# The MLP of a four-layer vision kernel by Strassen's product, in blocks of 256 pixels

## Chip, cores, metric

One core of one Trainium2 chip. The metric is the device time of one execution in microseconds, median of several runs. A ratio is the mean time of one kernel's fast runs over that of the other's fast runs of the same rounds, so it is not quite the ratio of the medians.

## The reference, cut to what matters

Four layers on `x` of shape (2, 512, 32, 32), all in f32: a deformable attention block with an MLP, then three attention layers. The change touches the MLP, which ends the first layer:

```python
xn2 = _bn(x, bn2_g, bn2_b)
h1 = jax.nn.gelu(jnp.einsum('bchw,oc->bohw', xn2, mlp_w1) + mlp_b1[None, :, None, None], approximate=False)
return x + jnp.einsum('bchw,oc->bohw', h1, mlp_w2) + mlp_b2[None, :, None, None]
```

512 channels go to 2048 and back, for 2 x 1024 = 2048 pixels.

## The kernel before

The MLP runs in four halves of 512 pixels. Channels lie on the 128 partitions, so 512 channels are CC = 4 chunks and 2048 are 16. `wa` and `wb` hold the two weights. `norm` is the group norm of layer 1, advanced in steps between MLP groups, so that layer 1 can start at once.

```python
xn = normed(0, 0)                                  # GpSimd: 4 tensor_scalar
for b in range(B):
    for half in range(2):
        ...
        h1 = one.tile([P, HID // P, HALF], F32, name="hid")
        for m in range(HID // P):                  # 16 groups of 4 matmuls
            ph = ps.tile([P, HALF], F32, name="ph")
            for k in range(CC):
                nc.tensor.matmul(
                    ph, w1[:, k, m * P : (m + 1) * P], xn_now[:, k, :], start=(k == 0), stop=(k == CC - 1)
                )
            nc.scalar.activation(h1[:, m, :], ph, AF.Gelu, bias=col("mlp_b1", m))
            if b == 1 and m % 4 == 3:
                advance(norm)
        ...
        for m in range(CC):                        # 4 groups of 16 matmuls
            pp = ps.tile([P, HALF], F32, name="pp2")
            for k in range(HID // P):
                nc.tensor.matmul(
                    pp, w2[:, k, m * P : (m + 1) * P], h1[:, k, :], start=(k == 0), stop=(k == HID // P - 1)
                )
            nc.vector.scalar_tensor_tensor(
                xs[b][:, m, n], pp, col("mlp_b2", m), xs[b][:, m, n], ALU.add, ALU.add
            )
            nc.sync.dma_start(out=x_d[b, m, :, n], in_=xs[b][:, m, n])
```

Around it, the pool `chan` has 9 buffers of 4 KB a partition in SBUF, the core's working memory. Each holds 128 channels of one image: of the normalised images of layers 1 and 2 (four buffers an image) or of the attention heads' outputs. The fold weights `g2`, `v2` and the bias row `vbias` have a place from the start.

Of the kernel before, what the change touches and what calls it, by code (L numbers as in the profile page):

```python
# [11 lines left out]
F32 = mybir.dt.float32  # L12
AF = mybir.ActivationFunctionType
ALU = mybir.AluOpType
# [4 lines left out]
P = 128  # L19
B, C, H, W = 2, 512, 32, 32  # L20
HW = H * W
CC = C // P
HALF = 512
# [5 lines left out]
HID = 4 * C  # L29
# [50 lines left out]
def kernel(ctx: ExitStack, tc: tile.TileContext, a: dict, out: bass.AP):  # L80
    nc = tc.nc
# [10 lines left out]
    def col(name, i=0, n=1):  # L92
        lo = _PC_AT[name][0] + i
        return pc[:, lo : lo + n]
# [7 lines left out]
    xs = []  # L102
# [26 lines left out]
    def advance(steps, n=1):  # L129
        for _ in range(n):  # L130
            next(steps, None)

    def accumulate(pm, pairs):
        for k, (w, m) in enumerate(pairs):
            nc.tensor.matmul(pm, w, m, start=(k == 0), stop=(k == len(pairs) - 1))  # L135
# [759 lines left out]

            attend([(k[:DH], q[:DH])], 1.0, vT, [(m * P, P) for m in range(CC)], store)

    def layers(f, g2, v2, t2_b, o2_b):


        f.enter_context(in_order(tc))
        small = f.enter_context(tc.tile_pool(name="small", bufs=2))
        keep = f.enter_context(tc.tile_pool(name="keep", bufs=1))
        chan = f.enter_context(tc.tile_pool(name="chan", bufs=9))
        ps_m = f.enter_context(tc.tile_pool(name="ps_m", bufs=2, space=PSUM))


        vb = keep.tile([P, 3, CC], F32, name="vb")
        with nc.allow_non_contiguous_dma("1536 numbers"):
            nc.sync.dma_start(out=vb, in_=a["vb"].rearrange("l (k p) -> p l k", p=P))  # L910
        vbias = keep.tile([P, C], F32, name="vbias")
        nc.sync.dma_start(out=vbias, in_=a["vb"][0].partition_broadcast(P))
        gb3 = keep.tile([P, CC], F32, name="gb3")
        nc.vector.tensor_scalar(gb3, vb[:, 2, :], col("gamma3"), None, ALU.mult)
        ones = keep.tile([P, P], F32, name="ones1")
# [60 lines left out]
        wb = wb_stack.enter_context(tc.tile_pool(name="wb", bufs=1, side="right"))  # L976
        (w2,) = load_w(wb, "wb", [a["mlp_w2"]])
        with ExitStack() as mlp:
            one = mlp.enter_context(tc.tile_pool(name="mlp1", bufs=1, side="right"))
            two = mlp.enter_context(tc.tile_pool(name="mlp2", bufs=2, side="right"))  # L980
            ps = mlp.enter_context(tc.tile_pool(name="mlp_ps", bufs=3, space=PSUM))

            def normed(b, half):
                n = slice(half * HALF, (half + 1) * HALF)
                xn = two.tile([P, CC, HALF], F32, name="xn2")
                for cc in range(CC):
                    nc.gpsimd.tensor_scalar(  # L987
                        xn[:, cc, :], xs[b][:, cc, n], s2[:, cc : cc + 1], col("bn2_b", cc), ALU.mult, ALU.add
                    )
                return xn  # L990

            xn = normed(0, 0)
            for b in range(B):
                for half in range(2):
                    n = slice(half * HALF, (half + 1) * HALF)
                    xn_now = xn
                    if (b, half) != (B - 1, 1):
                        xn = normed(*divmod(2 * b + half + 1, 2))
                    h1 = one.tile([P, HID // P, HALF], F32, name="hid")
                    for m in range(HID // P):  # L1000
                        ph = ps.tile([P, HALF], F32, name="ph")
                        for k in range(CC):
                            nc.tensor.matmul(  # L1003
                                ph, w1[:, k, m * P : (m + 1) * P], xn_now[:, k, :], start=(k == 0), stop=(k == CC - 1)
                            )
                        nc.scalar.activation(h1[:, m, :], ph, AF.Gelu, bias=col("mlp_b1", m))  # L1006
                        if b == 1 and m % 4 == 3:
                            advance(norm)
                    if (b, half) == (B - 1, 1):
                        qkv1, proj1 = load_w(wa, "wa", [a["qkv1_w"], a["proj1_w"]])  # L1010
                    for m in range(CC):
                        pp = ps.tile([P, HALF], F32, name="pp2")
                        for k in range(HID // P):
                            nc.tensor.matmul(  # L1014
                                pp, w2[:, k, m * P : (m + 1) * P], h1[:, k, :], start=(k == 0), stop=(k == HID // P - 1)
                            )
                        nc.vector.scalar_tensor_tensor(  # L1017
                            xs[b][:, m, n], pp, col("mlp_b2", m), xs[b][:, m, n], ALU.add, ALU.add
                        )
                        nc.sync.dma_start(out=x_d[b, m, :, n], in_=xs[b][:, m, n])  # L1020
                if b == 0:
                    for w, j in ((g2, 0), (v2, 1)):
                        nc.sync.dma_start(out=w, in_=fold_d[j])
        drain(norm)


# [87 lines left out]
            return r  # L1114

        wb_stack.close()

        vp = f.enter_context(tc.tile_pool(name="vp", bufs=1))
        pp_ = f.enter_context(tc.tile_pool(name="pp", bufs=4))
# [40 lines left out]
        for i in range(65):  # L1160
# [17 lines left out]
            if late is not None:  # L1178

                lb, lm, ls, lp = late  # L1180
                if ls == 0:
                    pv = ps_v.tile([P, HW], F32, name="pv")
                    if lm == 0 and lb == 1:
                        vT = new_v()
                        drain(values(qkv1[:, :, 2 * C : 3 * C], h1s[1], vT, bias=vbias))
                for half in range(2):
                    n = slice(half * HALF, (half + 1) * HALF)
                    for part in range(2):
                        lo = lm * P + part * 64
                        nc.tensor.matmul(  # L1190
                            pv[part * 64 : part * 64 + 64, n],
                            vT[:, ls, lo : lo + 64],
                            lp[:, part, n],
                            start=(ls == 0),
                            stop=(ls == 7),
                        )
                if ls == 1:
                    acc = accp.tile([P, 2, HW], F32, name="acc")
                    summed(acc, lp, p_first)
                elif ls > 1:  # L1200
                    summed(acc, lp, None)
                p_first = lp
                if ls == 7:
                    o = chan.tile([P, HW], F32, name="o", tag="chan")
                    nc.vector.tensor_copy(o, pv)
                    drain(dividing)
                    dividing = divide(o, acc)
                    os_[lb].append(o)
                    if lm == 3 and lb == 0:
                        more = chain([None] * 6, add_projection(xs[0], proj1, "proj_b", os_[0]))  # L1210
# [52 lines left out]
        for b in range(B):  # L1263
# [5 lines left out]
            ps = []  # L1269
# [68 lines left out]
    t2_b, o2_b = [const.tile([P, CC], F32, name=name) for name in ("t2_b", "o2_b")]  # L1338
    with ExitStack() as l0:
        w1 = layer0(l0, fold_d, t2_b, o2_b)  # L1340
    with tc.tile_pool(name="fold2", bufs=1) as pool, ExitStack() as fast:
        g2, v2 = [pool.tile([P, CC, C], F32, name=name) for name in ("g2", "v2")]
        layers(fast, g2, v2, t2_b, o2_b)
    bad = nc.values_load(flag[0:1, 0:1], min_val=0, max_val=P)
    with tc.If(bad != 0):
        with ExitStack() as g:
# [86 lines left out]
```

## Time and profile before

| | before |
|---|---|
| median of 4 runs (lowest to highest) | 3701.33 us (3700.52 to 3702.98) |
| TensorE busy, share of the span | 99% |
| MLP, first matmul to first matmul after it | 440.1 us |
| MLP matmul records (see below), us apart | 1024, 0.429 |
| VectorE, ScalarE busy in the MLP | 19 us, 50 us |

One f32 matmul stands in the trace as two records with a weight load each. A record lasts longer (592 ns at 512 pixels) than the distance to the next one's start (429 ns), so neighbours overlap. What a record costs is the distance between starts. The lines themselves are in the prediction below.

### The profile page before, as it was taken

How to read it: one execution, taken by the hardware profiler on the slowest of the kernel's cores; microseconds unless marked ns; L12 is line 12 of the kernel's file. 1: busy time of each engine (PE TensorE's matmuls, PEld its weight loads, DVE VectorE, ACT ScalarE, POOL GpSimd, SP SyncE). 2: the span in 40 equal slices, each digit the busy share in tenths (PEclk: the TensorE clock that was granted, in tenths of full speed). 3: DMA queues.
4: the chain of work that ended last, by engine and by line, in shares of the span. 5: the costliest groups of instructions: out<-in, count | busy, mean ns of one | idle time of the engine just before them, and what ended most of it. 6: DMA issues, size and time to landing. Idle time of an engine off the chain costs nothing.

```text
span 3702.9 us, 37416 instructions
## 1 busy us (share of the span) xinstructions
PE 3677.3 (99%) x15234; PEld 1339.8 (36%) x15234; DVE 2369.3 (64%) x2317; ACT 1588.3 (43%) x1964; POOL 500.1 (14%) x189
## 2 busy tenths in 40 slices
PE   9999999999999999999999999999999999999999
PEld 4333333333333333333333334444433333444443
DVE  6998998998996998998999950000046356030222
ACT  3656566566664566666656541110134233111111
POOL 1123122122131011131132300000001000000000
PEclk9999999999999999999999999999999999999999
DMA  4010112111010010010001001000100000000000
GB/s 150 16 21 17 18 24 62 16 21 18 19 23 12 16 21 18 20 22 16 21 18 24 18 1 54 9 32 12 57 0 1 1 1 1 14 1 0 6 29 24
DMA packets 96853, 78.42 MB, mean 21 GB/s; under 512 B 10657, under 2 KB 84769, under 8 KB 95905
## 3 DMA queue, kind: packets, MB, share of 16 engines
q1 hardware_dynamic: 96528, 75.41, 8.2%
q8 instruction: 123, 2.02, 0.2%
q10 hardware_dynamic: 144, 0.52, 0.0%
q14 instruction: 58, 0.47, 0.0%
HBM read 64.12 MB, written 10.75 MB: 20 GB/s over the span
## 4 chain that ended last, share of the span: by engine, by line
PE 98%; DVE 1%; ACT 0%; DMA 0%; issue 0%; POOL 0%; SPq 0%; DVEq 0%; POOLq 0%; ACTq 0%
PE z L454 48%; PE sim L476 6%; PE pw L135 6%; PE ph L1003 6%; PE pp L1014 6%; PE pm L1038 5%; PE pmv L135 5%; PE score L1142 3%; PE score L135 3%; PE pv L1190 3%; PE ppr L1069 2%; PE pp L561 2%; PE pf L135 1%; PE pk L135 0%; DVE acc L1080 0%; PE pv L539 0%
## 5 line engine op out<-in xcount | busy, mean ns | idle before, releaser
L454 PE MATMUL z<-h,cpb_w 128*64 128x512 f32 x8192 | 1791.0, 594 | 3.5 <-ACT qpad L273 3.5
L462 ACT ACTIVATE h<-z,b2h 128x1024 f32<-128x1024 f32 x1024 | 1140.0, 1115 | 840.6 <-PE z L454 834.7
L436 DVE CUSTOM_DVE_ANT_1 h<-tab,tab 128x1024 f32<-128x1024 f32 x1024 | 1220.3, 1232 | 113.8 <-PE z L454 113.3
L454 PEld LDWEIGHTS z<-h,cpb_w 128*64 128x64 f32 x8192 | 574.3, 137 | 1183.0 <-issue 1085.1
L467 DVE SCALAR_TENSOR_TENSOR h<-h,turn,h 128x1024 f32<-128x1024 f32 x512 | 688.0, 1344 | 5.3 <-ACT h L462 5.3
L421 POOL TENSOR_SCALAR tab<-tab,pc 128x512 f32<-128x512 f32 x63 | 294.8, 4679 | 1621.7 <-DMA tab<-slog_d 1309.4
L1017 DVE SCALAR_TENSOR_TENSOR x<-pp,pc,x 128x512 f32<-128x512 f32 x16 | 12.0, 752 | 375.7 <-PE pp L1014 375.7
L476 PE MATMUL sim<-h,w 128*32 128x512 f32 x2048 | 234.4, 595 | 0.7 <-DVE h L467 0.7
L135 PE MATMUL pw<-p,vT 128*128 128x512 f32 x512 | 221.8, 593 | 1.3 <-DVE y L1248 1.3
L1003 PE MATMUL ph<-xn,wa 128*128 128x512 f32 x512 | 220.9, 592 | 1.4 <-POOL xn L987 1.4
L1014 PE MATMUL pp<-hid,wb 128*128 128x512 f32 x512 | 220.4, 592 | 0.0
L1143 ACT ACTIVATE p<-score 128x1024 f32<-128x1024 f32 x144 | 139.5, 1021 | 156.7 <-PE score L1142 156.7
L1080 DVE TENSOR_TENSOR acc<-acc,p 128x2048 f32<-128x2048 f32 x56 | 129.6, 2314 | 105.1 <-ACT p L1143 57.8
L1006 ACT ACTIVATE hid<-ph,pc 128x512 f32<-128x512 f32 x64 | 44.0, 687 | 332.6 <-PE ph L1003 332.6
L965 POOL TENSOR_SCALAR hc<-x,sc,sh 128x1024 f32<-128x1024 f32 x16 | 29.6, 1862 | 902.2 <-DVE sh L961 870.1
L1082 DVE TENSOR_TENSOR acc<-p 128x2048 f32<-128x2048 f32 x12 | 27.5, 2291 | 183.4 <-ACT p L1277 110.0
L1003 PEld LDWEIGHTS ph<-xn,wa 128*128 128x128 f32 x512 | 97.0, 190 | 123.2 <-issue 120.5
L1014 PEld LDWEIGHTS pp<-hid,wb 128*128 128x128 f32 x512 | 97.3, 190 | 122.5 <-issue 122.5
L135 PEld LDWEIGHTS pw<-p,vT 128*128 128x128 f32 x512 | 97.0, 190 | 122.6 <-issue 121.0
L422 POOL TENSOR_SCALAR tab<-tab,pc 128x512 f32<-128x512 f32 x63 | 129.1, 2049 | 20.8 <-DMA tab<-slog_d 20.6
L1142 PE MATMUL score<-q,k 64*128 64x512 f32 x512 | 127.2, 615 | 0.0
L1038 PE MATMUL pm<-hc,wa 128*64 128x512 f32 x512 | 122.4, 603 | 0.0
(217 smaller groups left out, 2050.1 us busy)
## 6 DMA issues: line engine op xcount, KB each, us to landing
tab<-slog_d SPq DMA_DIRECT2D x128, 256.0 KB, 6.5
wa<-in_qkv_w SPq DMA_DIRECT2D x8, 768.0 KB, 6.7
xt<-in_xt SPq DMA_DIRECT2D x8, 512.0 KB, 3.9
wa<-in_mlp_w SPq DMA_DIRECT2D x4, 1024.0 KB, 15.9
wb<-in_mlp_w SPq DMA_DIRECT2D x16, 256.0 KB, 5.4
x_d<-x SPq DMA_DIRECT2D x16, 256.0 KB, 2.0
out<-x SPq DMA_DIRECT2D x16, 256.0 KB, 2.0
wa<-in_proj_w SPq DMA_DIRECT2D x8, 256.0 KB, 8.8
```

What stands on the lines that cost most here:

```text
L135: nc.tensor.matmul(pm, w, m, start=(k == 0), stop=(k == len(pairs) - 1))
L421: engine.tensor_scalar(tabs[0], tabs[0], col("cpb_w1", 0), col("cpb_b1"), ALU.mult, ALU.add)
L436: nc.vector._custom_dve(TENSOR_ADD_SAT, out=h1, in0=tx[:, quad, ri, :].unsqueeze(1).to_broadcast([P, H, W]), in1=ty[:, quad, ri, :].unsque ...
L454: nc.tensor.matmul(z[point * 64 : point * 64 + 64, n], cpb_w2[:, part * 64 : part * 64 + 64], h1s[point][:, n], start=True, stop=True,)
L462: nc.scalar.activation(h2, z, AF.Relu, bias=b2h[:, part : part + 1])
L467: nc.vector.scalar_tensor_tensor(parts[0], parts[0], turn, parts[1], ALU.mult, ALU.add)
L476: nc.tensor.matmul(sim[quad * 32 : quad * 32 + 32, n], w3[:, lo : lo + 32], h2[:, n], start=(r == 0 and j < 4), stop=False,)
L1003: nc.tensor.matmul(ph, w1[:, k, m * P : (m + 1) * P], xn_now[:, k, :], start=(k == 0), stop=(k == CC - 1))
L1014: nc.tensor.matmul(pp, w2[:, k, m * P : (m + 1) * P], h1[:, k, :], start=(k == 0), stop=(k == HID // P - 1))
L1038: nc.tensor.matmul(pm[at : at + wide], w[:, k, lo + at : lo + at + wide], h[k][:, n], start=(k == 0), stop=(k == CC - 1),)
L1142: nc.tensor.matmul(sc[:, part, :], ks[part][r, left[part]], qs[part][r, n], start=True, stop=True)
L1143: nc.scalar.activation(p[:, :, n], sc, AF.Exp, scale=scale)
```

## The change

Strassen's product (in Winograd's form) multiplies 2 x 2 block matrices with 7 block products in place of 8, for additions on other engines. The intent is to give TensorE, which is busy all the time, one eighth less MLP work. Blocks are 256 pixels wide, halved into 128, so each moving operand is 128 wide.

- The sums of weights are formed once on VectorE, in place where possible, while the first block is multiplied plainly.
- The order of the second product is chosen for the wait between the two products: product 1 is taken for both output halves over seven chunks, and the chunk that comes last only then.
- Room is made in SBUF: `chan` goes to 4 buffers, the heads' outputs get 5 of their own, and `g2`, `v2`, `vbias` are loaded after the MLP.

The diff, cut to its core:

```diff
-        chan = f.enter_context(tc.tile_pool(name="chan", bufs=9))
+        chan = f.enter_context(tc.tile_pool(name="chan", bufs=4))
...
+            def lefts(w, name):          # sums of a weight's blocks
+                    engine.tensor_tensor(t1[c], a21[c], a22[c], ALU.add)
+                    engine.tensor_tensor(t2[c], t1[c], a11[c], ALU.subtract)
+                    engine.tensor_tensor(a21[c], a11[c], a21[c], ALU.subtract)
+                    engine.tensor_tensor(t4[c], a12[c], t2[c], ALU.subtract)
...
+            def rights(v, name):         # sums of the pixels' blocks: 4 tensor_tensor alike
...
+                at = {1: a[:, 0], 2: a[:, 1], 6: a[:, 2], 3: a[:, 3], 4: b[:, 0], 5: b[:, 1], 7: b[:, 2]}
...
+            def combined(pms, p1, lower):
+                nc.vector.tensor_tensor(upper, a[:, 1:3], twice(p1), ALU.add)
+                nc.vector.tensor_tensor(u, b[:, 1:3], twice(upper[:, 1]), ALU.add)
+                nc.vector.tensor_tensor(lower, b[:, 0:2], twice(u[:, 1]), ALU.add)
+                nc.vector.tensor_tensor(upper[:, 1], a[:, 3], u[:, 0], ALU.add)
...
+            for blk in range(1, NBLK):
...
+                for c in range(MC + 1):
+                    if c < MC:
+                        pms = products(left1, right1, slice(c * P, (c + 1) * P), (1, 2, 6, 7, 5, 4, 3))
+                        p1 = first_of(pms)
+                    if c:
+                        activated(c - 1, upper)
+                    if c < MC:
+                        upper = combined(pms, p1, hid[:, MC + c, :].rearrange("p (j n) -> p j n", j=2))
+                    if c:
+                        form_right2(slice(c - 1, c))
+                    if b == 1 and c % 4 == 3:
+                        advance(norm)
...
+                both = [products(left2, right2, cols[c], ()) for c in range(2)]
+                for ks in (range(MC - 1), range(MC - 1, MC)):
+                    for c in range(2):
+                        for k in ks:
+                            nc.tensor.matmul(both[c][0][:, 0], left2[0][:, k, cols[c]], right2[0][:, k, :], ...)
+                for c in range(2):
+                    products(left2, right2, cols[c], (2, 6, 7, 5, 4, 3), both[c])
...
+        fold2 = f.enter_context(tc.tile_pool(name="fold2", bufs=1))   # vbias, g2, v2: loaded after the MLP
+        outs = f.enter_context(tc.tile_pool(name="outs", bufs=5))
```

`a` and `b` are two banks of PSUM, the memory that TensorE writes its sums to, with room for four results of 128 pixels each. There are three of each, and each is one tile of the program. A *group* is one pass of `c`: the seven products for one pair of column blocks, 14 matmuls or 28 records. The *seam* is the place where the second product of a block follows on the first.

More of the change, by code (lines that the diff above doesn't have):

```diff
@@ L896, in general, with layers @@
             attend([(k[:DH], q[:DH])], 1.0, vT, [(m * P, P) for m in range(CC)], store)
-    def layers(f, g2, v2, t2_b, o2_b):
+    def layers(f, fold_d, t2_b, o2_b):
         f.enter_context(in_order(tc))
@@ L910, in layers @@
             nc.sync.dma_start(out=vb, in_=a["vb"].rearrange("l (k p) -> p l k", p=P))
-        vbias = keep.tile([P, C], F32, name="vbias")
-        nc.sync.dma_start(out=vbias, in_=a["vb"][0].partition_broadcast(P))
         gb3 = keep.tile([P, CC], F32, name="gb3")
@@ L981, in layers, with blocks @@
             ps = mlp.enter_context(tc.tile_pool(name="mlp_ps", bufs=3, space=PSUM))
-            def normed(b, half):
-                n = slice(half * HALF, (half + 1) * HALF)
-                xn = two.tile([P, CC, HALF], F32, name="xn2")
+            BLK = 256
+            PX = BLK // 2
+            def blocks(v, k, n):
+                return [
+                    [v[:, i * k // 2 : (i + 1) * k // 2, j * n // 2 : (j + 1) * n // 2] for j in range(2)]
+                    for i in range(2)
+                ]
@@ new lines, in lefts, with form @@
+            def lefts(w, name):
+                k, n = w.shape[1:]
+                (a11, a21), (a12, a22) = blocks(w, k, n)
+                t1, t2, t4 = [one.tile([P, k // 2, n // 2], F32, name=f"{name}s{i}") for i in (1, 2, 4)]
+                def form(engine, cols):
+                    c = (slice(None), slice(None), cols)
+                    engine.tensor_tensor(t1[c], a21[c], a22[c], ALU.add)
+                    engine.tensor_tensor(t2[c], t1[c], a11[c], ALU.subtract)
+                    engine.tensor_tensor(a21[c], a11[c], a21[c], ALU.subtract)
+                    engine.tensor_tensor(t4[c], a12[c], t2[c], ALU.subtract)
+                return (a11, a12, t4, a22, t1, t2, a21), form
@@ new lines, in rights, with form @@
+            def rights(v, name):
+                k, n = v.shape[1:]
+                (b11, b12), (b21, b22) = blocks(v, k, n)
+                t1, t2, t4 = [one.tile([P, k // 2, n // 2], F32, name=f"{name}t{i}") for i in (1, 2, 4)]
+                def form(chunks):
+                    c = (slice(None), chunks, slice(None))
+                    nc.vector.tensor_tensor(t1[c], b12[c], b11[c], ALU.subtract)
+                    nc.vector.tensor_tensor(t2[c], b22[c], t1[c], ALU.subtract)
+                    nc.vector.tensor_tensor(b12[c], b22[c], b12[c], ALU.subtract)
+                    nc.vector.tensor_tensor(t4[c], b21[c], t2[c], ALU.subtract)
+                return (b11, b21, b22, t4, t1, t2, b12), form
@@ new lines, in product, with products @@
+            def product(pm, i, left, right, cols):
+                l, r = left[i - 1], right[i - 1]
+                accumulate(pm, [(l[:, k, cols], r[:, k, :]) for k in range(l.shape[1])])
+            def products(left, right, cols, some, pms=None):
+                if pms is None:
+                    pms = [ps.tile([P, 4, PX], F32, name=f"pm{i}") for i in "ab"]
+                a, b = pms
+                at = {1: a[:, 0], 2: a[:, 1], 6: a[:, 2], 3: a[:, 3], 4: b[:, 0], 5: b[:, 1], 7: b[:, 2]}
+                for i in some:
+                    product(at[i], i, left, right, cols)
+                return pms
@@ new lines, in combined, with twice @@
+            def combined(pms, p1, lower):
+                a, b = pms
+                upper = two.tile([P, 2, PX], F32, name="upper")
+                u = two.tile([P, 2, PX], F32, name="u")
+                def twice(v):
+                    return v.unsqueeze(1).to_broadcast([P, 2, PX])
+                nc.vector.tensor_tensor(upper, a[:, 1:3], twice(p1), ALU.add)
+                nc.vector.tensor_tensor(u, b[:, 1:3], twice(upper[:, 1]), ALU.add)
+                nc.vector.tensor_tensor(lower, b[:, 0:2], twice(u[:, 1]), ALU.add)
+                nc.vector.tensor_tensor(upper[:, 1], a[:, 3], u[:, 0], ALU.add)
+                return upper.rearrange("p j n -> p (j n)")
@@ L986, in normed, with first_of @@
+            def first_of(pms):
+                p1 = two.tile([P, PX], F32, name="p1")
+                nc.scalar.copy(p1, pms[0][:, 0])
+                return p1
+            left1, form1 = lefts(w1, "w1")
+            left2, form2 = lefts(w2, "w2")
+            def normed(blk):
+                b, n = blk * BLK // HW, slice(blk * BLK % HW, blk * BLK % HW + BLK)
+                xn = one.tile([P, CC, BLK], F32, name="xn2")
                 for cc in range(CC):
@@ L990, in normed @@
                 return xn
-            xn = normed(0, 0)
-            for b in range(B):
-                for half in range(2):
-                    n = slice(half * HALF, (half + 1) * HALF)
-                    xn_now = xn
-                    if (b, half) != (B - 1, 1):
-                        xn = normed(*divmod(2 * b + half + 1, 2))
-                    h1 = one.tile([P, HID // P, HALF], F32, name="hid")
-                    for m in range(HID // P):
-                        ph = ps.tile([P, HALF], F32, name="ph")
-                        for k in range(CC):
-                            nc.tensor.matmul(
-                                ph, w1[:, k, m * P : (m + 1) * P], xn_now[:, k, :], start=(k == 0), stop=(k == CC - 1)
-                            )
-                        nc.scalar.activation(h1[:, m, :], ph, AF.Gelu, bias=col("mlp_b1", m))
-                        if b == 1 and m % 4 == 3:
-                            advance(norm)
-                    if (b, half) == (B - 1, 1):
-                        qkv1, proj1 = load_w(wa, "wa", [a["qkv1_w"], a["proj1_w"]])
-                    for m in range(CC):
-                        pp = ps.tile([P, HALF], F32, name="pp2")
-                        for k in range(HID // P):
-                            nc.tensor.matmul(
-                                pp, w2[:, k, m * P : (m + 1) * P], h1[:, k, :], start=(k == 0), stop=(k == HID // P - 1)
-                            )
-                        nc.vector.scalar_tensor_tensor(
-                            xs[b][:, m, n], pp, col("mlp_b2", m), xs[b][:, m, n], ALU.add, ALU.add
-                        )
-                        nc.sync.dma_start(out=x_d[b, m, :, n], in_=xs[b][:, m, n])
-                if b == 0:
-                    for w, j in ((g2, 0), (v2, 1)):
-                        nc.sync.dma_start(out=w, in_=fold_d[j])
@@ new lines, in normed_rights, with added @@
+            def normed_rights(blk):
+                right, form = rights(normed(blk), "xn")
+                form(slice(0, CC // 2))
+                return right
+            NBLK = B * HW // BLK
+            MC = HID // P // 2
+            def added(blk, m, src):
+                b, at = blk * BLK // HW, blk * BLK % HW
+                x = xs[b][:, m, at : at + BLK]
+                nc.vector.scalar_tensor_tensor(x, src, col("mlp_b2", m), x, ALU.add, ALU.add)
+                nc.sync.dma_start(out=x_d[b, m, :, at : at + BLK], in_=x)
@@ new lines, in layers @@
+            xn = normed(0)
+            hid = one.tile([P, HID // P, BLK], F32, name="hid")
+            for c in range(MC):
+                for m in (MC + c, c):
+                    pm = ps.tile([P, BLK], F32, name="pmp", tag="pma")
+                    accumulate(pm, [(w1[:, k, m * P : (m + 1) * P], xn[:, k, :]) for k in range(CC)])
+                    nc.scalar.activation(hid[:, m, :], pm, AF.Gelu, bias=col("mlp_b1", m))
+                form1(nc.vector, slice(c * P, (c + 1) * P))
+            right1 = normed_rights(1)
@@ new lines, in layers, with activated @@
+            for m in (2, 3, 0, 1):
+                pm = ps.tile([P, BLK], F32, name="pmp2", tag="pmb")
+                accumulate(pm, [(w2[:, k, m * P : (m + 1) * P], hid[:, k, :]) for k in range(HID // P)])
+                added(0, m, pm)
+                if m >= 2:
+                    form2(nc.vector, slice((m - 2) * P, (m - 1) * P))
+            for blk in range(1, NBLK):
+                b = blk * BLK // HW
+                hid = one.tile([P, HID // P, BLK], F32, name="hid")
+                right2, form_right2 = rights(hid, "hid")
+                def activated(c, upper):
+                    nc.scalar.activation(hid[:, MC + c, :], hid[:, MC + c, :], AF.Gelu, bias=col("mlp_b1", MC + c))
+                    nc.scalar.activation(hid[:, c, :], upper, AF.Gelu, bias=col("mlp_b1", c))
+                upper = None
+                for c in range(MC + 1):
[10 more added lines that the diff above has]
+                        advance(norm)
+                if blk + 1 < NBLK:
+                    right1 = normed_rights(blk + 1)
+                else:
+                    qkv1, proj1 = load_w(wa, "wa", [a["qkv1_w"], a["proj1_w"]])
+                cols = [slice(c * P, (c + 1) * P) for c in range(2)]
+                both = [products(left2, right2, cols[c], ()) for c in range(2)]
+                for ks in (range(MC - 1), range(MC - 1, MC)):
+                    for c in range(2):
+                        for k in ks:
+                            nc.tensor.matmul(
+                                both[c][0][:, 0],
+                                left2[0][:, k, cols[c]],
+                                right2[0][:, k, :],
+                                start=(k == 0),
+                                stop=(k == MC - 1),
+                            )
+                for c in range(2):
+                    products(left2, right2, cols[c], (2, 6, 7, 5, 4, 3), both[c])
+                    lower = two.tile([P, 2, PX], F32, name="lower")
+                    upper = combined(both[c], first_of(both[c]), lower)
+                    added(blk, 2 + c, lower.rearrange("p j n -> p (j n)"))
+                    added(blk, c, upper)
@@ L1116, in layers @@
         wb_stack.close()
+        fold2 = f.enter_context(tc.tile_pool(name="fold2", bufs=1))
+        vbias = fold2.tile([P, C], F32, name="vbias")
+        nc.sync.dma_start(out=vbias, in_=a["vb"][0].partition_broadcast(P))
+        g2, v2 = [fold2.tile([P, CC, C], F32, name=name) for name in ("g2", "v2")]
+        for w, j in ((g2, 0), (v2, 1)):
+            nc.sync.dma_start(out=w, in_=fold_d[j])
+        outs = f.enter_context(tc.tile_pool(name="outs", bufs=5))
         vp = f.enter_context(tc.tile_pool(name="vp", bufs=1))
@@ L1203, in layers @@
                 if ls == 7:
-                    o = chan.tile([P, HW], F32, name="o", tag="chan")
+                    o = outs.tile([P, HW], F32, name="o")
                     nc.vector.tensor_copy(o, pv)
@@ L1340 @@
         w1 = layer0(l0, fold_d, t2_b, o2_b)
-    with tc.tile_pool(name="fold2", bufs=1) as pool, ExitStack() as fast:
-        g2, v2 = [pool.tile([P, CC, C], F32, name=name) for name in ("g2", "v2")]
-        layers(fast, g2, v2, t2_b, o2_b)
+    with ExitStack() as fast:
+        layers(fast, fold_d, t2_b, o2_b)
     bad = nc.values_load(flag[0:1, 0:1], min_val=0, max_val=P)
```

## The prediction

> **What bounds the kernel now.** I read the page first: the busy shares and the slices, then the groups. TensorE is busy 99% of the span at a granted clock of 0.998, so time is won only where TensorE gets less to do, and only while nothing starts to hold it up.
>
> ```profile
> span 3702.9 us, 37416 instructions
> PE 3677.3 (99%) x15234; PEld 1339.8 (36%) x15234; DVE 2369.3 (64%) x2317; ACT 1588.3 (43%) x1964; POOL 500.1 (14%) x189
> ...
> L1003 PE MATMUL ph<-xn,wa 128*128 128x512 f32 x512 | 220.9, 592 | 1.4 <-POOL xn L987 1.4
> L1014 PE MATMUL pp<-hid,wb 128*128 128x512 f32 x512 | 220.4, 592 | 0.0
> ```
>
> The two last lines are the MLP. Each has 256 matmuls of 512 pixels, and each matmul stands as two records (x512). A record takes 592 ns, but they overlap: busy time over count gives 431 ns. The chain that ended last, in order of time, shows the stage as one unbroken TensorE chain; its first and last pieces:
>
> ```profile
> 2224.27 55.17 PE ph L1003 x128
> 2279.44 54.93 PE pp L1014 x128
> ...
> 2609.49 54.93 PE pp L1014 x128
> 2664.42 13.88 PE pm L1038 x64
> ```
>
> So the MLP takes 2664.4 - 2224.3 = **440.1 us**, 429 ns a record. The table of windows shows how idle the rest is there (columns: PE, PEld, DVE, ACT, POOL, then clock, DMA share, GB/s):
>
> ```profile
> 2224.20:2664.40 440.20, 440.13 (x1030) 194.97 (x1030) 19.45 (x42) 49.52 (x70) 15.78 (x19) 1.00 0.09 34
> ```
>
> VectorE works 19 of 440 us. Strassen's form trades TensorE time for VectorE time, and here that is free until VectorE's share per group nears TensorE's.
>
> **What the skill says.** (1) The Trainium skill, "TensorE: Matmul & The Clock Gate", section "LDWEIGHTS (loading the stationary operand)": a weight load costs its columns over 1.2 per ns, 107 ns for 128 columns; "Back-to-back issue gap" says that spacing is set by load and matmul together. The change makes every moving operand 128 wide, where this matters. The trace has such a run, eight chained 128-wide matmuls of another stage:
>
> ```profile
> 220.19 1.86 PEld L135 LDWEIGHTS pk<-wy,xt 128*128 128x128 f32 x16 [0.81 <-issue]
> 221.98 0.30 PEld L135 LDWEIGHTS pk<-cst,wsum 128*128 128x128 f32 x2
> ```
>
> Sixteen loads start within 221.98 - 220.19 = 1.79 us: **112 ns a record**, against 429/4 = 107 ns if time fell exactly with width. The page's load figure agrees to 5%; its 81 ns for N=128 is not this f32 form. (2) "VectorE: DVE Perf Modes", "Why `tensor_tensor` can't do 2×_2P or 4×" and "Why PSUM operands drop a tier": f32 tensor_tensor stays at one element a cycle. The trace agrees: 682 ns for 512 elements and 280 ns for 128, so 1.05 ns an element and 146 ns fixed. (3) "PSUM — Partial Sum Buffer", "PSUM bank collisions raise a hardware error": engines must be kept apart by bank, not by address. I take it that readers of the products therefore wait for a bank's last product; no run here shows that yet. (4) "ScalarE: Activation LUTs", "What ACT_TABLE_LOAD costs": 1283 ns a load; the trace has 1.28 us.
>
> **The change, part by part.** *TensorE work.* A block of 256 pixels takes 7 products instead of 8. First MLP product: 8 column groups x 7 products x 2 chunks = 112 matmuls of 128 pixels; second: 2 x 7 x 8 = 112. Seven blocks: 7 x 224 = 1568 matmuls = 3136 records x 0.112 = **351 us**. The plain first block: 128 matmuls of 256 pixels, 256 records at half of 429 ns (estimate) = **55 us**. Sum 406 against 440: **-34 us**. Of the 1/8 saved on 7/8 of the stage (-48 us), 14 us go back because 128-wide records pace at 112 and not 107 ns.
>
> *VectorE work beside it.* Per group of the first product: three tensor_tensor of 256 elements (0.146 + 256 x 1.05 ns = 0.41 us each), one of 128 (0.28), then four of 128 to form the right operands of the second product: 1.24 + 0.28 + 1.12 = 2.64 us. Dependent VectorE operations in the group norm follow each other some 0.035 us after the end of the last; with these gaps I take 2.86 us. TensorE takes 28 x 0.112 = 3.13 us. VectorE is 91% loaded, and stays just under. ScalarE has a copy of 128 (0.27) and two Gelus of 256 (0.42 each, between 309 ns for 128 and 1050 for 1024): 1.1 us. The sums of weights are formed in block 0: 32 operations of 0.41 us and 8 of 1.22 us = 23 us beside 55 us of matmuls, hidden. The second product has 25 us of TensorE per block and some 10 us of VectorE, hidden. The next block's normalised pixels are made in it, too.
>
> *The seam between the products.* After the last group ends (T), by bank: first-product copy to T+0.5, four VectorE operations to T+2.3, Gelus to T+2.9. TensorE has 14 matmuls that do not need that chunk, until T+3.13. So the reordering just covers the chain; about 0.3 us a block may show. The operands formed from the last chunk come at T+4.7 and are wanted at T+5.4 or later.
>
> *Group norm inside.* In blocks 4 to 7 a step of layer 1's norm goes to VectorE at the fourth and eighth group: two statistics (0.67 each) and a small one, 1.6 us. At 0.27 us of slack a group, half a microsecond of lag may reach the seam. The step with the logarithm, the exponential and three table loads costs more:
>
> ```profile
> 2595.69 0.16 DVE L935 COPY var<-pg 128x4 f32<-128x4 f32 x1 [13.20 <-PE pg L933]
> ...
> 2600.52 0.16 DVE L961 TENSOR_TENSOR sh<-pc,sh 128x4 f32<-128x4 f32 x1
> ```
>
> It holds VectorE 2600.7 - 2595.7 = 5.0 us, now in block 7's fourth group; 4 x 0.27 = 1.1 us is recovered, so some 4 us arrive on TensorE. Stalls: 1 (start) + 6 x 0.3 + 4 = **+7 us**.
>
> *After the MLP.* The next weights (4 MB) now have 25 us of matmuls to hide in, not 55; the 4 MB of the second MLP weight landed some 15 us after its first issue, so this stays hidden. The fold weights and the bias row load later, but are wanted 15 us or more after. The pool for normalised images shrinks from 9 buffers to 4, so image 1's cannot be made ahead:
>
> ```profile
> 2792.77 7.56 POOL L965 TENSOR_SCALAR hc<-x,sc,sh 128x1024 f32<-128x1024 f32 x3 [187.25 <-DVE sh L961]
> 2832.47 3.33 POOL L965 TENSOR_SCALAR hc<-x,sc,sh 128x1024 f32<-128x1024 f32 x1 [32.14 <-PE pm L1038]
> ```
>
> Three ran 40 us early and one waited for a buffer. Now all four wait for 2832; two are wanted some 4 us later and take 5 to 6.7 us: **+2 us**.
>
> Sum: -34 + 7 + 2 = -25 us, so 3701.6 - 25 = **3676 us**.
>
> **Rivals.** *VectorE becomes the bound of the first product.* For: 2.86 against 3.13 us a group is thin, and broadcast operands or waits between VectorE and ScalarE could add 0.5 us. Against: the durations are this trace's, and three PSUM buffers a tag smooth single delays. If a group took 3.6 us, 56 groups x 0.5 = 28 us would be lost: some 3704 us, no gain. *All of it hides.* With stages tracked by product, not bank, and no stall anywhere, only the pace counts: 3701.6 - 34 = 3668 us. If the longer chains also paced at 107 ns, 3136 x 5 ns = 15 us more: 3653 us; 112 ns in every such run of the trace speaks against it. *A switch cost at each product.* Were each of the (56 + 14) x 7 = 490 products to cost 0.1 us of restart, 49 us would be added: 3725 us. Against: four separate matmuls of 128 elsewhere in the trace keep the 112 ns across their starts. *The late loads show.* If the next weights came 10 us late, 3686 us.
>
> **Range and chances.** The TensorE sum is firm to some 5 us; the stalls may be 0 to 25 us, more above than below. That gives 3664 to 3700. Faster by 2% needs -74 us, more than Strassen's whole -48 us: 1%. Slower by 2% needs +74 us, which takes two rivals together: 2%. Within 2%: 97%.
>
> **What would show it.** Right: 128-wide MLP records 112 ns apart; the stage about 413 us long; VectorE over 80% busy in the first products and below half in the second; TensorE's idle time sitting at the seams, most in the last block, released by ScalarE's Gelu. Wrong: TensorE waiting in every group for PSUM released by VectorE, records apart by other than 112 ns, tensor_tensor of 256 well over 0.41 us, or waits for the loads after the stage.

## The result, and the profile after

The changed kernel takes **3667.99 us** (3667.32 to 3670.42, 4 runs) against 3701.33 us. The ratio is 0.9911, 95% interval 0.9893 to 0.9928: 33 us less, a gain of 0.9%. The prediction was 3676 with a range of 3664 to 3700 and 97% on "within 2%".

From the chain that ended last in the changed kernel, its first block and the start of the next stage (start, us, what):

```profile
2220.83 55.49 PE pmp L135 x256
...
2308.61 5.36 PE pmb L135 x48
...
2629.00 13.88 PE pm L1161 x64
```

The middle line is a run of narrow records: 5.36 us / 48 = 112 ns each. The stage now takes 2629.0 - 2220.8 = 408.2 us (408.1 from start to start), where it took 440.1: **32 us less**. That is the gain. The two traced executions differ by more, 3702.9 - 3665.5 = 37.4 us. The rest is not the change's. TensorE ran at half clock in two stretches of the traced execution of the kernel before that the other doesn't have. The stretches, with the granted clock third from the end; first before, then after:

```profile
70.00:78.00 8.00, 6.42 (x22) 2.04 (x24) 5.36 (x7) 5.25 (x5) 0.35 (x1) 0.79 0.00 1
3116.00:3126.00 10.00, 7.82 (x22) 2.58 (x19) 7.53 (x4) 1.17 (x2) 0.00 (x0) 0.83 0.00 0
```

```profile
70.00:78.00 8.00, 8.00 (x38) 2.73 (x40) 7.96 (x11) 6.12 (x6) 0.00 (x0) 1.00 0.00 0
3080.00:3090.00 10.00, 7.82 (x26) 2.78 (x23) 8.37 (x4) 1.72 (x3) 0.00 (x0) 1.00 0.00 0
```

The first pair lies in front of the MLP, where the programs are the same: there TensorE waited 1.6 us longer in the kernel before (3.5 us against 1.9) and then ran at half clock, 3.4 us lost together. The second pair holds the same wait of 2.18 us in layer 2 in both kernels; from its end to the end of the program the kernel before took 1.9 us longer. Such stretches last 3.41 us, and within a trace they start whole multiples of 3.413 us apart. On that grid the wait in the kernel before (3117.08 to 3119.26) lies inside one window (3116.79 to 3120.21); in the changed kernel (3081.66 to 3083.85) a border at 3082.67 cuts it into 1.0 and 1.2 us, and no stretch follows. So two to five microseconds between two traces of this program depend on where a wait happens to fall. Below, the stage's own length is read beside the time.

How one group of the first product now runs (start, us, engine, what; other lines left out):

```profile
2295.17 0.27 ACT L1056 COPY p<-pma 128x128 f32<-128x128 f32 x1 [2.06 <-PE pma L135]
2295.33 0.51 ACT L1107 ACTIVATE hid<-hid,pc 128x256 f32<-128x256 f32 x1
2295.47 0.42 DVE L1048 TENSOR_TENSOR upper<-pma,p 128x256 f32<-128x256 f32 x1 [0.66 <-ACT p L1056]
...
2295.93 0.42 DVE L1049 TENSOR_TENSOR u<-pmb,upper 128x256 f32<-128x256 f32 x1
...
2296.39 0.42 DVE L1050 TENSOR_TENSOR hid<-pmb,u 128x256 f32<-128x256 f32 x1
...
2296.73 0.28 DVE L1051 TENSOR_TENSOR upper<-pma,u 128x128 f32<-128x128 f32 x1
2296.92 0.28 DVE L1018 TENSOR_TENSOR hidt<-hid 128x128 f32<-128x128 f32 x1
...
2297.24 0.29 DVE L1019 TENSOR_TENSOR hidt<-hid,hidt 128x128 f32<-128x128 f32 x1
2297.45 0.28 DVE L1020 TENSOR_TENSOR hid<-hid 128x128 f32<-128x128 f32 x1
...
2297.65 0.28 DVE L1021 TENSOR_TENSOR hidt<-hid,hidt 128x128 f32<-128x128 f32 x1
...
2298.59 0.42 DVE L1048 TENSOR_TENSOR upper<-pma,p 128x256 f32<-128x256 f32 x1 [0.66 <-ACT p L1056]
```

VectorE works from 2295.47 to 2297.93 = 2.46 us of the 3.13 us of a group (28 records; 2298.59 - 2295.47 = 3.12), and waits 0.66 us for TensorE through ScalarE's copy. TensorE never waits here. An operation that needs the one just ahead starts 0.03 us after its end (2295.93). One that doesn't starts some 0.08 us *before* that end (2297.45, 0.21 us after the start at 2297.24).

All that TensorE waited for in the stage (engine, line, waited for, us in total, times, longest):

```profile
PE pmp L135 <- POOL xn L1066: 1.4, 1, 1.4
...
PE pma L1134 <- ACT hid L1108: 0.8, 2, 0.5
```

The first is the start, as it was before. The second is the last block, where the long step of the group norm sits.

### The profile page after: what moved, and what is told of

Read it like the earlier page. It is cut to its first block, busy times and chain, and to the rows that moved or that the text cites. A ratio compares the mean times of both kernels' runs of the same rounds, so it can differ in the third digit from the quotient of the medians.

```text
span 3665.5 us, 43059 instructions
## 1 busy us (share of the span) xinstructions
PE 3640.8 (99%) x17602; PEld 1544.3 (42%) x17602; DVE 2555.0 (70%) x2905; ACT 1614.9 (44%) x2098; POOL 499.3 (14%) x205
## 4 chain that ended last, share of the span: by engine, by line
PE 98%; DVE 1%; ACT 1%; issue 0%; DMA 0%; POOL 0%; SPq 0%; DVEq 0%; POOLq 0%; ACTq 0%
PE z L454 48%; PE sim L476 6%; PE pw L135 6%; PE pm L1161 5%; PE pma L135 5%; PE pmv L135 5%; PE pmb L135 4%; PE score L1272 3%; PE score L135 3%; PE pv L1320 3%; PE ppr L1192 2%; PE pp L561 2%; PE pmp L135 2%; PE pf L135 1%; PE pma L1134 1%; PE pk L135 0%
## 5 line engine op out<-in xcount | busy, mean ns | idle before, releaser
L1056 ACT COPY p<-pma 128x128 f32<-128x128 f32 x70 | 18.6, 265 | 304.2 <-PE pma L135 304.2
L1048 DVE TENSOR_TENSOR upper<-pma,p 128x256 f32<-128x256 f32 x70 | 29.5, 422 | 163.6 <-ACT p L1056 163.5
L476 PEld LDWEIGHTS sim<-h,w 128*32 128x32 f32 x2048 | 60.8, 109 | 159.4 <-issue 156.6
L1320 PE MATMUL pv<-p,vT 128*64 128x512 f32 x512 | 121.4, 595 | 0.0
L135 PE MATMUL score<-t,hc 128*128 128x512 f32 x256 | 110.2, 592 | 0.0
L1378 DVE TENSOR_TENSOR y<-pw,r 128x512 f32<-128x512 f32 x32 | 21.8, 682 | 115.9 <-PE pw L135 115.9
```

Source lines behind the costliest of these rows:

```text
L135: nc.tensor.matmul(pm, w, m, start=(k == 0), stop=(k == len(pairs) - 1))
L476: nc.tensor.matmul(sim[quad * 32 : quad * 32 + 32, n], w3[:, lo : lo + 32], h2[:, n], start=(r == 0 and j < 4), stop=False,)
L1320: nc.tensor.matmul(pv[part * 64 : part * 64 + 64, n], vT[:, ls, lo : lo + 64], lp[:, part, n], start=(ls == 0), stop=(ls == 7),)
```

## The experiments

Eleven runs on three chips, each beside runs of the kernel before. All of them gave correct results. "The stage" is read from the start of the first MLP matmul to the start of the first matmul after it: 440.1 us before, 408.1 after.

**The width alone: `plain128` and `plain256`.** The kernel before with each MLP matmul cut by pixels, no Strassen:

```diff
-                        for k in range(CC):
-                            nc.tensor.matmul(ph, w1[:, k, m * P : (m + 1) * P], xn_now[:, k, :], ...)
+                        for q in range(0, HALF, 128):      # or 256; the second product alike
+                            accumulate(ph[:, q : q + 128], [(w1[...], xn_now[:, k, q : q + 128]) for k in range(CC)])
```

> The kernel before, with every MLP matmul cut into four of 128 pixels: the same arithmetic, no Strassen, only the width. Theory (128-wide f32 records with a weight load each pace at 111.65 ns and not at a quarter of 428.6): 4096 records x 111.65 = 457.3 us in place of 438.9, 18 us more, 3720. Rival (the 112 ns belong to something else in the changed kernel, such as its switching of banks): no more than 3 us more.

Measured: 3721.41 us against 3701.15, ratio 1.0055 (1.0038 to 1.0072), stage 460.9 us. Where nothing waits and the clock is full, the 4096 records stand 111.67 ns apart in the mean, 457 us in all; 1.7 us more is a stretch at half clock at the stage's start. The theory holds. Narrowing to 128 costs 20 us when all of the MLP is done so, some 18 of them by the spacing, with nothing of Strassen in it.

> The kernel before, with every MLP matmul cut into two of 256 pixels. Theory (at 256 the load of 190 ns hides under a matmul of 214 ns): 2048 records x 214.5 ns, within 2 us of the kernel before, 3701. Rival (a fixed cost of 4 to 5 ns a record at every width): 2048 - 1024 more records x 4.5 ns = 5 us more, 3706.

Measured: 3704.19 us, ratio 1.0009 (0.9992 to 1.0026), stage 443.3 us. Records stand 215.9 ns apart. That is between the theory and the rival: not free, but less than 4.5 ns a record. The 429.17 ns at 512 and the 215.86 at 256 fit a part in proportion to the width and 2.5 ns for each record. The same sum gives 109.2 at 128; the other 2.5 ns of the 111.67 come only there. What they are isn't shown.

**The buffers and late loads alone: `buffers_only`.** The kernel before with the change's pools and loads, and the MLP as it was:

```diff
-        chan = f.enter_context(tc.tile_pool(name="chan", bufs=9))
+        chan = f.enter_context(tc.tile_pool(name="chan", bufs=4))
...  # vbias, g2, v2 loaded after the MLP; o from a pool of 5, as in the change
```

> The kernel before with only the other part of the change: four buffers for the normalised images and five for the heads' outputs in place of nine shared, and the fold weights and the bias row loaded after the MLP. The prediction gave this 2 us more, 3703. The trace of the changed kernel shows TensorE waiting for none of it: then 3701, within 1 us, and no wait of TensorE for the normalised images or the bias row.

Measured: 3701.87 us against 3701.15, ratio 1.0003 (0.9987 to 1.002), and TensorE's waits are those of the kernel before. Nothing is lost here. The lines of the changed kernel show why (GpSimd, and TensorE at the place):

```profile
2797.04 4.51 POOL L963 TENSOR_SCALAR hc<-x,sc,sh 128x1024 f32<-128x1024 f32 x2 [195.68 <-PE pm L1161]
2802.55 4.50 POOL L963 TENSOR_SCALAR hc<-x,sc,sh 128x1024 f32<-128x1024 f32 x2 [1.00 <-PE pm L1161]
```

```profile
2801.28 1.94 PE L1161 MATMUL pm<-hc,wa 128*64 128x512 f32 x8
2806.78 1.94 PE L1161 MATMUL pm<-hc,wa 128*64 128x512 f32 x8
```

GpSimd does wait for TensorE to leave the buffers, as predicted. But they come free two at a time, 5.5 us apart (2797.04 and 2802.55). The matmuls at 2801.28 still end a sum of image 0. The first that wait for GpSimd's semaphore are those at 2806.78, 9.7 us after the first buffers came free, and the two buffers that they read are filled by 2801.55. The next two are filled by 2807.05 and wanted at 2813.14.

**The seam: `natural_order`.** The second product in its plain order:

```diff
-                both = [products(left2, right2, cols[c], ()) for c in range(2)]
-                for ks in (range(MC - 1), range(MC - 1, MC)):
-                    ...
                 for c in range(2):
-                    products(left2, right2, cols[c], (2, 6, 7, 5, 4, 3), both[c])
+                    both = products(left2, right2, cols[c], (1, 2, 6, 7, 5, 4, 3))
```

> The changed kernel with the seam undone: the second product of each block takes all seven products of its first half, then all of its second, the last hidden chunk in its turn. Theory (the seam is a chain of copy, four VectorE operations and two Gelus that ends some 2.8 us after the last matmul of the first product, as the trace of the changed kernel shows at 2301.17 to 2304.00): the last chunk is now wanted after 7 matmuls of 0.223 us = 1.56 us, so TensorE waits about 1.3 us for ScalarE's Gelu in each of seven blocks, 9 us in all, and the time is about 3677. Rival (the chunk is ready by then, or the wait is hidden by something else): no waits over 0.1 us, 3668.

Measured: 3680.5 us, ratio 0.9945 (0.9928 to 0.9961), stage 419.0 us, 11 us longer. All of TensorE's waits for the chunk, and the one of block 1:

```profile
PE pma L135 <- ACT hid L1108: 8.5, 8, 1.9
```

```profile
2301.54 1.86 PE L135 MATMUL pma<-hid,wb 128*128 128x128 f32 x14
...
2303.88 0.49 ACT L1108 ACTIVATE hid<-upper,pc 128x256 f32<-128x256 f32 x1
...
2304.43 1.27 PE L135 MATMUL pma<-hid,wb 128*128 128x128 f32 x9 [1.02 <-ACT hid L1108]
```

Fourteen records run, then TensorE waits 1.02 us for the Gelu that ends at 2304.37. The theory holds, the rival falls. The reordering is worth 8.5 - 0.8 = 7.7 us of waits. The last block's wait also brought a stretch of 3.4 us at half clock, which cost 1.7 us more. The other 1.5 us of the 11 lie at the waits, too: a wait costs more than its idle time, since a record of 275 ns then no longer overlaps the next. At block 1's, two starts stand 1300 and 214 ns apart where undisturbed ones stand 112: 1.29 us for 1.02 us of idle.

**Waits by bank: `bank_first` and `natural_bank_first`.** The products of a group in another order, so that the first bank is complete earlier:

```diff
-                        pms = products(left1, right1, slice(c * P, (c + 1) * P), (1, 2, 6, 7, 5, 4, 3))
+                        pms = products(left1, right1, slice(c * P, (c + 1) * P), (1, 2, 6, 3, 7, 5, 4))
```

> The changed kernel with the products of a first-product group in the order 1, 2, 6, 3, 7, 5, 4, so that the bank with products 1, 2, 6, 3 is finished 12 records = 1.34 us before the group's end. Theory (readers wait for the last product of a bank): the copy of the first product starts about 1.25 us before the group's last matmul ends, where it now starts 0.1 us after it; the time stays within 2 us of 3668, since nothing waited for this. Rival (readers wait for the whole group, both banks): the copy still starts after the group's end. Rival for the time (VectorE holds TensorE back unseen): some us faster.

Measured: 3669.27 us, ratio 0.9913 (0.9897 to 0.993), stage 407.4 us. At block 1's last group:

```profile
2301.18 0.27 ACT L1056 COPY p<-pma 128x128 f32<-128x128 f32 x1 [2.06 <-PE pma L135]
...
2301.82 0.61 PE L135 MATMUL pmb<-xnt,wa 128*128 128x128 f32 x4
2302.27 3.40 PE L1134 MATMUL pma<-hid,wb 128*128 128x128 f32 x29
```

The group's last product ends at 2301.82 + 0.61 = 2302.43, and the copy starts 1.25 us before it. In the changed kernel it starts after the group. So readers wait for the last product of a bank, neither for their own nor for the group's. (Each bank is one tile of the program here, so the run can't tell a wait by bank from a wait by tile.) The time did not move. The stage is 0.7 us shorter: at the seams of blocks 1 to 5 the changed kernel has two records 149 and 213 ns apart, 0.14 us lost each time, and here they are gone.

> Both edits at once. Theory (the length of the chain behind the last group is what TensorE waits for): with one bank done early the copy and the first VectorE operation move ahead of the group's end and the last Gelu ends about 1.9 us after it, so the wait at each seam is about 0.35 us, some 2 to 3 us in all, time about 3671, 6 us less than the natural order alone. Rival (the wait is set by something else, such as the operands formed from the last chunk): the same waits as with the natural order alone.

Measured: 3672.74 us, ratio 0.9923 (0.9906 to 0.9939), stage 412.4 us. TensorE waits 4.1 us in all: 0.35 us at block 1's seam, and 2.0 in the last block. That is 6.5 us of stage and 8 us of time less than `natural_order`. The same chain, shortened, shortens the same wait; the rival falls.

**VectorE's slack: `vector_plus2` and `vector_plus6`.** More VectorE work in each group, into a tile that nobody reads:

```diff
+                        for i in range(2):        # or 6
+                            nc.vector.tensor_tensor(idle[:, i % 3], p1, p1, ALU.add)
```

> The changed kernel with two more VectorE operations of 128 elements in each group of the first product, into a tile that nobody reads. Theory (VectorE has 0.66 us to spare in a group of 3.13 us): two operations 0.205 us apart make 2.47 + 0.41 = 2.88 us, under TensorE's 3.13, and the time stays within 3 us of 3668. Rival (VectorE already sets the pace of the groups): 56 groups x 0.41 = 23 us more, 3691.

Measured: 3671.52 us, ratio 0.9922 (0.9905 to 0.9938), stage 410.0 us. The groups keep their 3.13 us. TensorE's waits rise from 0.8 to 2.6 us, all in the last block behind the group norm. The rival's 23 us aren't there. In median the time is 3.5 us up and so a little outside of what was expected; 1.9 us of it is in the stage, and the trace has the stretch at half clock in layer 2 (1.7 us) that the changed kernel's lacks.

> As vector_plus2, with six more operations in each group. Theory: 2.47 + 6 x 0.205 = 3.70 us a group, over TensorE's 3.13 by 0.57; eight groups a block make 4.6 us, less about 1 us of slack in the first group and before the seam, so 3.5 us in each of seven blocks: about 25 us more, 3693 (20 to 35 us more), with TensorE waiting at the seams or for a PSUM buffer. Rival (VectorE does not matter here at all): 3668.

Measured: 3701.54 us, ratio 1.0004 (0.9987 to 1.002), 34 us up: all of Strassen's gain is gone. A group now takes VectorE 3.59 us (3.70 expected), and TensorE waits:

```profile
PE pma L1137 <- ACT hid L1109: 14.8, 11, 2.1
PE pma L1137 <- DVE idle L1121: 5.7, 3, 2.2
PE pma L1137 <- DVE upper L1051: 2.6, 1, 2.6
```

The waits sum to 23 us. Four of them were followed by 3.4 us at half clock, 1.7 us each, which makes 30 of the stage's 32 us. So the first rival of the prediction is a real limit: 0.41 us more a group was borne, 1.1 us was not, and by the trace 0.66 us is free.

**A candidate: `after_again`, `first_block_too`, `first_block_bank`.** The runs show that TensorE's records set the time and that VectorE has room. The first block's second product can then go by Strassen as well, if the second weight's sums are formed during its first product:

```diff
-            for m in (2, 3, 0, 1):
-                pm = ps.tile([P, BLK], F32, name="pmp2", tag="pmb")
-                ...
+                if c:
+                    form_right2(slice(c - 1, c))
+                if c < MC - 2:
+                    form1(nc.vector, slice(c * P, (c + 1) * P))
+                elif c == MC - 2:
+                    form2(nc.vector, slice(0, P))
+            ...                                   # the rest of form2 and form1, then
+            second_product(0, right2)             # the loop's second product as a function
```

> The changed kernel as it is, once more beside the two below: 3668, within 2 us. In its trace the first block's second product is 128 records of 216 ns = 27.6 us.

> A candidate: the first block's second product by Strassen as well; the sums of the second weight are formed during the block's first product (its first half) and at the start of the second, some sums of the first weight later. Theory (TensorE's work sets the time wherever VectorE fits beside it): 27.6 us become 224 records x 111.7 = 25.0 us, so 2.6 us less, about 3665.5, with no new wait of TensorE over 1 us. Rival (VectorE, with 8 operations of 1.2 us and the right operands besides the first weight's sums, is late for the seam of the first block): TensorE waits there and nothing is won.

> The same candidate with the products of a first-product group ordered by bank (1, 2, 6, 3, 7, 5, 4). The stage of the bank-first kernel was 0.7 us shorter in its trace than the changed kernel's; so about 3665, at most 1 us less than the candidate without it. Rival (the order matters for nothing that TensorE waits for): the same.

Measured in the same rounds, the kernel before at 3701.97 us:

| | median, us | ratio (95%) | stage, us |
|---|---|---|---|
| `after_again` | 3668.89 | 0.9910 (0.9896 to 0.9924) | 408.1 |
| `first_block_too` | 3667.22 | 0.9904 (0.9889 to 0.9920) | 405.5 |
| `first_block_bank` | 3665.88 | 0.9901 (0.9885 to 0.9916) | 404.8 |

The stage became 2.6 us shorter, as the records count, and with the bank order another 0.7 us, with no new wait. The times follow, but the intervals overlap. Run against run the candidates come out lower: the slowest `first_block_bank` (3667.21) is under the fastest `after_again` (3667.71), though the changed kernel reached 3667.32 in its first rounds. The candidates are faster in the trace of the stage; by the times it is likely for `first_block_bank` and not shown for `first_block_too`.

## Why the prediction was right

The time lay inside the range and the class was the likely one. The class tests little: no gain at all would also have been within 2%. The mechanism is the predicted one, and the gain was 33 us in place of 25. By the steps:

1. **TensorE's work, -34 us.** Right. The 3136 narrow records stand 111.67 ns apart, 350 us, and the 256 of the first block 215.8 ns, 55 us: 405.4 against 406. `plain128` shows the price of the width by itself. The estimate "half of 429" for 256 pixels was 1.3 ns low. The prediction set the 112 ns beside 107 ns for a load. That the load sets the pace isn't shown: a load's record lasts 190 ns at 512 and 256 and 192 at 128, while the spacing goes from 429 to 112.
2. **VectorE beside it.** The verdict is right, the number was too high: 2.46 us a group, not 2.86. The durations were as read (0.42 and 0.28 us). The mis-sized term is the gap between operations. I put 0.035 us behind nearly all, but those that do not need the one ahead start 0.08 us before its end. The slack is 0.66 us, not 0.27. `vector_plus2` and `vector_plus6` bracket it. The predicted busy share over 80% in the first product was also too high: 79% within a full group, 64% over block 1's first product.
3. **The seam.** Right in length. The last Gelu ends 2.83 us after the second product's first record in `natural_order` (2304.37 - 2301.54), for 2.9 predicted, though a Gelu of 256 took 0.50 us and not my 0.42. Of the 0.3 us a block 0.14 showed, and not at the chunk that I had in mind: the records 149 and 213 ns apart come twelve records into the second product, where the seventh chunk is wanted (2302.54), just as its Gelu ends (2302.49). The eighth is ready at 2304.00 and wanted at 2304.43. `natural_order` gives the value of the reordering.
4. **Stalls, +7 us.** Mis-sized, and the largest miss. Of the stage's 408.1 us, 405.4 are records, and all the rest is 2.7 us. The 1 us for the start should not have been counted: that wait is 1.4 us in both kernels and lies in front of the stage. The group norm's long step held VectorE less long, from 2592.67 to 2596.16 in the last block, 3.5 us and not 5.0, since the first of its table loads ran from 2591.07, before VectorE had come to it. And with 0.66 us of slack a group the lag was mostly worked off before the seam: 0.8 us reached TensorE where 4 were predicted.

```profile
2592.67 0.15 DVE L933 COPY var<-pg 128x4 f32<-128x4 f32 x1
...
2596.00 0.16 DVE L959 TENSOR_TENSOR sh<-pc,sh 128x4 f32<-128x4 f32 x1
```

5. **After the MLP, +2 us.** Wrong. The wait for the buffers exists but ends in time; `buffers_only` shows no loss. I had all four buffers come free at once and two of them wanted some 4 us later. They come free in twos, and the first two are wanted 9.7 us later; the matmuls some 4 us later (2836.70 in the kernel before) are image 0's last.
6. **Rivals.** VectorE as bound: not reached, but near. A restart cost at each product: none; the spacing holds across products. Late loads: no wait of TensorE for them. "All of it hides" gave 3668, which is what was measured, but that is partly luck: its reason (tracking by product) did not hold in `bank_first`, and the stage itself won 32 us and not 34.

Points 1, 4 and 5 explain 7 of the 8 us between prediction and result (0.6 + 4.3 + 2). The remaining 1 us is within what stretches at half clock move from run to run.

## What to carry to other kernels

Where TensorE is the bound and VectorE idle, Strassen's form pays, but count the records at their real spacing: a quarter of the width cost 26% and not 25% of the time, which took 14 of the 48 us. Compare the other engine's time per group with TensorE's, operations that follow without a dependence counted at less than their duration (here 0.21 us for 0.28), and ask how far the lag of an occasional long step is worked off before a place where TensorE needs the result. Behind each change of stage, give TensorE work that needs no last result; here 14 reordered matmuls saved 8 us of waits.

## What the Trainium skill lacked or had wrong

- "TensorE: Matmul & The Clock Gate", "Back-to-back issue gap": it has no row for f32, and no page of the skill gives a spacing for it. Here an f32 matmul is two records, each 429.2, 215.9 and 111.67 ns apart at 512, 256 and 128 pixels. An estimate from the page, twice its N/2.4 plus its fixed 2.5 ns once, gives 429.2 and 215.8, which agrees; at 128 it gives 109.2 and 111.67 was measured. The page's sustained 131 ns at 512 and 81 ns at 128 fit none of these runs.
- The same page, "What's actually happening": the clock is said to fall to half after at least one idle window of about 3.4 us. Here a window need not be idle throughout: TensorE went to half clock for 3.41 us after windows with 2.0 to 2.4 us of waiting in them (four times in `vector_plus6`, once in `natural_order`). Two waits of 2.17 us in `vector_plus6`, each cut by a window's border into at most 1.66 us, brought none. Over all thirteen traces, from 60 us to 3660 us, twelve of the thirteen stretches follow a window with 1.99 us of waiting or more (idle times over 50 ns added up), and no such window went without; in front of the thirteenth, in `plain128`, it was 1.58 us.
- "VectorE: DVE Perf Modes", "The DRAIN you can't avoid": it says that the next operation waits for an empty pipe, and that one that isn't held starts earlier; the section gives no size for that (the skill has one elsewhere; a pointer is missing). Here independent f32 tensor_tensor of 128 elements start 0.21 us apart with a duration of 0.28 us, and dependent ones 0.03 us after the end.
- "ScalarE: Activation LUTs", "What ACT_TABLE_LOAD costs": the load of 1.28 us is right, but the further drain of 1380 ns was not seen. In the kernel before a load starts at 2596.28 and the activation at 2597.57, and the operation ahead of the load ends at 2596.26.
